# A graph layer on one core: VectorE's work of a step in one fixed order, the spares' slots from one shifted row, and two running extremes

## The chip, the cores and the metric

The kernel runs on one core of one Trainium2 chip. The metric is device time in microseconds (us): the median of the timed runs, 1736.52 us for the kernel before. A profile comes from one execution, whose own time stands beside it.

## The reference, cut to what matters

```python
# N = 12500 nodes, 128 features, E = 400000 edges sorted by dst, edge_type 0 or 1
Xs = x[src]
msg = where(edge_type == 0, Xs @ W_data.T + b_data, Xs @ W_control.T + b_control)
agg = segment_sum(msg, dst, N)
x = layernorm(x + relu(agg + (x @ W_self.T + b_self)))
```

## The kernel before

Sums come first and weights afterwards: for every node the rows of `x` of its incoming edges are added up by edge type, and only these two sums are multiplied by the weights. Rows are held as three bfloat16 parts (`x3` in SBUF, `rows3` in DRAM). The edges are cut into 25 groups of 125 chunks of 128 edges. In a group there are five windows; each has 5 "p" chunks, whose rows GpSimd gathers by indirect DMA (`msg`, L828), and 20 "e" chunks, whose rows are picked out of `x3` by TensorE. A step `w` of the main loop (L1177) handles one such set of 20 e-chunks; there are 107 steps. In a step TensorE does the following, in five units `t` (`picked`, L909):

- it picks rows (`got`, L929) with a one-hot matrix `pick`, ScalarE copies them out as `emsg` (L943), and TensorE adds them up by destination (`sums`, L755), with a one-hot matrix `esel` that VectorE makes in three parts of 10, 9 and 6 cells (1760, 1584 and 1056 elements, `choose`, L918). The tiles `esel` have two buffers;
- in between it adds up the gathered rows with `psel`, counts (L859) and, once a group, multiplies finished sums by the weights (L1048).

Work for later steps runs beside this. For step `w + 2` the slots of the edges are found: each edge has a cell (block of 128 nodes) and needs its rank among the step's edges in that cell. VectorE makes `O` (which cell) and, from `O`, two sums `few` of tens and fives of chunks (L612, L613) and `same` (equal cells in a lane, L602). TensorE counts what lies ahead (`side`, L622). Then comes the **ranks' chain** on VectorE: `ahead` (L630), the product (L634), two folds (L639), `found` (L641), `rank` (L643), `rm` (L533), `rv` (L674). TensorE puts the edges into their slots (`put`, L686), ScalarE copies the result (`cell`, L694), and two DMAs bring it to DRAM and back to all partitions as `pick` (L699), which VectorE turns into the one-hot matrix in the next step (L741). Edges that find no slot are spares: `over` (L645) takes the largest seven of each partition (`key`, `top`, `over_n`, `bits`), TensorE counts over the partitions (L552), VectorE makes `om_all` (L558), TensorE turns it into indices (L562), once for two steps; GpSimd gathers these rows (`both`, L904).

The order of the work comes from three things. Each piece of a step has a place between 0 and 1, and `merged` (L146) records the pieces in the order of their places. The tile framework then orders each engine's queue by these records and by its own estimates of when operands are ready, so VectorE's queue is not simply the recorded order. `issue_after` keeps an instruction behind a named one; before, the work for step `w + 3` and `pick` are only kept behind `rv` (`placed`). Each engine works through its own queue in order.

Where a sum is added into the accumulators `acc` and `cnt` (L817) the column comes from a table: `place_of` (L802) loads ten values into VectorE's registers once a group. `prep` (L473) makes a group's codes and keeps four running extremes (`worst`, L499), which `check_all` (L1102) looks at after the loop.

Of the kernel before, what the change touches and what calls it, by code (L numbers as in the profile page):

```python
# [8 lines left out]
FP = mybir.dt.float32  # L9
# [197 lines left out]
def short_path(ctx, tc, const, ident, eps, wT, brow, bad, x, src, dst, etype, ws, bs, out):  # L207
# [159 lines left out]
    slot_col = keep.tile([P, TOP, OVF], BF, name="slot_col")  # L367
    nc.vector.tensor_copy(slot_col, iota([TOP, OVF], [[-1, TOP], [1, OVF]], 0, 0, "i5"))

    om_all = [keep.tile([P, TOP, 2, OVF], BF, name=f"om_all{k}") for k in range(2)]  # L370
# [15 lines left out]
    worst = keep.tile([P, 5, P], FP, name="worst")  # L386
    nc.vector.memset(worst, 0.0)
# [13 lines left out]
    def places_and_weights():  # L401
# [14 lines left out]
        nc.vector.tensor_reduce(worst[0:1, 4, 0:1], place[:, 0].rearrange("o g w -> o (g w)"), AX.X, OP.max)  # L416
# [56 lines left out]
    def prep(g):  # L473
# [3 lines left out]
        width, high, low = (bounds_of[:GC, v, k:k + 1] for k in range(3))  # L477
        sf = pre.tile([GC, P], FP, name="sf", bufs=1)
        rel = pre.tile([GC, 2, P], FP, name="rel", bufs=1)
# [9 lines left out]
        def rows():  # L489
            near = near_of(g, d)  # L490
            for k in range(2):
                nc.vector.tensor_scalar(rel[:, k], d, near[k], None, op0=OP.subtract)
            nc.vector.tensor_single_scalar(kind, t, 0.0, op=OP.not_equal)
            nc.vector.scalar_tensor_tensor(code[:, 1], kind, width, rel[:, 1], op0=OP.mult, op1=OP.add)
            nc.vector.scalar_tensor_tensor(code[:, 0], kind, float(PW), rel[:, 0], op0=OP.mult, op1=OP.add)
            for k, (most, least) in enumerate(((float(PW - 1), 0.0), (high, low))):
                for j, (end, op) in enumerate(((most, OP.max), (least, OP.min))):
                    w = worst[:GC, 2 * k + j, :]
                    nc.vector.scalar_tensor_tensor(w, rel[:, k], end, w, op0=OP.subtract, op1=op)  # L499
# [29 lines left out]
    def select(sel, col, code2):  # L529

        rows, n, width = sel.shape
        shape = [rows, n, width // 2, 2]
        nc.vector.tensor_tensor(  # L533
            sel.rearrange("p n (w t) -> p n w t", t=2),
            col[:rows].rearrange("p (o w t) -> p o w t", o=1, t=2).to_broadcast(shape),
            code2.rearrange("p n (o t) -> p n o t", o=1).to_broadcast(shape),
            op=OP.is_equal,
        )
        return sel
# [3 lines left out]
    def spare_slots(w, at):  # L543
# [12 lines left out]
        def over_matrix():  # L556
            for k in range(n):
                nc.vector.tensor_scalar(om[:, :, k, :], slot_col, both["before"][:, k:k + 1], None, op0=OP.is_equal)  # L558

        def turn():  # L560
            for j in range(TOP):
                nc.tensor.matmul(  # L562
                    at["rk"][:, col:col + 3 * n], om[:, j].rearrange("p k o -> p (k o)"), both["bits"][:, :, :n, j],
                    start=(j == 0), stop=(j == TOP - 1), skip_group_check=True,
                )

        def keep():
            got = at["rk"][:, col:col + 3 * n].rearrange("p (v k) -> p k v", k=n)
            part = two.tile([P, 2], FP, name="part")
            for k in range(n):  # L570
# [3 lines left out]
                    code, got[half, k, 2:3].rearrange("p (n o) -> p n o", o=1).to_broadcast(list(code.shape))  # L574
                )
                nc.scalar.copy(part[half], got[half, k, :2])
# [6 lines left out]
    def give_slots(w):  # L583
# [5 lines left out]
        def behind():  # L589
            return tc.issue_after(placed[0].ins) if w > 1 else ExitStack()  # L590

        def block_matrix():
            O = s["held"] = two.tile([P, EC * NCELL], BF, name="O")
            s["O"] = O.rearrange("p (c j) -> p c j", j=NCELL)
            select(s["O"], cell_cols[w % 2], blk2)

        def same_lane():
# [3 lines left out]
            with behind():  # L601
                nc.vector.tensor_tensor(  # L602
# [5 lines left out]
        def fours():  # L608
            s["prod"] = big.tile([P, EC, NCELL + EC], BF, name="prod")
            h = s["few"] = s["prod"][:, :, :NCELL]  # L610
            with behind():
                nc.vector.tensor_add(h[:, :2 * CQ], s["O"][:, :2 * CQ], s["O"][:, 2 * CQ:])  # L612
            nc.vector.tensor_add(h[:, 2 * CQ:3 * CQ], h[:, :CQ], h[:, CQ:2 * CQ])  # L613
# [13 lines left out]
        def ranks():  # L627
            ahead = two.tile([P, NCELL], BF, name="ahead")
            with nc.allow_low_precision(reason="whole numbers; those over 256 need not be exact"):
                nc.vector.tensor_reduce(  # L630
                    ahead, s["ahead"][:, :2 * NCELL].rearrange("p (k j) -> p j k", k=2), AX.X, OP.add
                )
            prod = s["prod"]
            nc.vector.tensor_tensor(  # L634
                prod[:, :, :NCELL], s["O"], ahead.rearrange("p (o j) -> p o j", o=1).to_broadcast([P, EC, NCELL]),
                op=OP.mult,
            )
            for h in ((NCELL + EC) // 2, (NCELL + EC) // 4):
                nc.vector.tensor_add(prod[:, :, :h], prod[:, :, :h], prod[:, :, h:2 * h])  # L639
            found = two.tile([P, EC], FP, name="found")  # L640
            nc.vector.tensor_reduce(found, prod[:, :, :h], AX.X, OP.add)  # L641
            rank = s["rank"] = two.tile([P, EC, 2], BF, name="rank")
            nc.vector.tensor_copy(rank, found.rearrange("p (c o) -> p c o", o=1).to_broadcast([P, EC, 2]))  # L643

        def over():  # L645
            key = two.tile([P, EC], FP, name="key")
            nc.vector.scalar_tensor_tensor(key, s["rank"][:, :, 0], CAP - 0.5, pk, op0=OP.is_ge, op1=OP.mult)
# [3 lines left out]
            nc.vector.max(both["top"][:, w % 2, :], key)  # L651
# [18 lines left out]
        def rank_matrix():  # L670
            rm = select(big.tile([P, EC, CAP], BF, name="rm"), rank_col, s["rank"])
            rv = s["rv"] = two.tile([P, EC, 2, CAP], BF, name="rv")
            shape = [P, EC, 2, CAP // 2, 2]
            placed[:] = [nc.vector.tensor_tensor(  # L674
                rv.rearrange("p c v (r t) -> p c v r t", t=2),
                rm.rearrange("p c (o r t) -> p c o r t", o=1, t=2).to_broadcast(shape),
                vals2.rearrange("p c v (o t) -> p c v o t", o=1).to_broadcast(shape),
                op=OP.mult,
            )]
# [49 lines left out]
        if w % 2:  # L729
            s["tiled"][5] = [lambda: (turn_codes(), own_before())]  # L730
            s["own_turn"] = own_turn
        return s, [(0.58, block_matrix), (0.6, fours), (0.66, same_lane)], [
            (0.1, before), (0.31, ranks), (0.35, rank_matrix), (0.75, over),
        ]

    def pick_matrix(w):

        def half(a, b):
            t = slots[w]["pick"][:, a:b].rearrange("p j r -> p (j r)")
            with tc.issue_after(placed[0].ins):  # L740
                nc.vector.tensor_scalar(t, t, lane_f, None, op0=OP.is_equal)  # L741
        return [(0.6, lambda: half(0, NCELL))]


    acc, added, parts_in, at_places = {}, [], {}, {}
# [56 lines left out]
    def place_of(g, i):  # L802

        parts_in[g] = parts_in.get(g, 0) + 1
        if g not in at_places:
            with tc.issue_after(added[-2].ins) if len(added) > 1 else ExitStack():
                _, at_places[g] = nc.values_load_multi_w_load_instructions(
                    raw["place"][0:1, g, :], engines=[nc.vector.engine], min_val=0, max_val=R - WMAX,
# [552 lines left out]
```

## Time and profile before

| what | value |
|---|---|
| median of 3 runs (lowest, highest) | 1736.52 us (1736.14, 1736.97) |
| the profiled execution, its own time | 1736.11 us |
| its span, first to last instruction | 1734.3 us |
| mean granted TensorE clock | 0.992 |
| TensorE (PE) busy | 1569.6 us, 91% |
| VectorE (DVE) busy | 1550.3 us, 89% |
| ScalarE (ACT), GpSimd (POOL) busy | 1246.5 us, 1292.2 us |
| PE in the first 60 us | 6.7 us busy |

A share of busy time is a mean over stages. The first 75 us load and split `x`; from then on all 107 steps look alike, with more work in those in which a group is prepared or finished. PE's busy time is modelled and takes in the 0.17 to 0.33 us that a matmul is on its way, so short waits do not show as idle time.

### The profile page before, as it was taken

Reading aid. Unit: us, or ns where it says so; the run is one execution under the profiler, and the core shown is the slowest. Engines: PE = TensorE matmul, PEld = TensorE weight load, DVE = VectorE, ACT = ScalarE, POOL = GpSimd, SP = SyncE. Lnnn points to the kernel's source line nnn. Section 1 sums busy time; section 2 is a strip of 40 time slices with the busy share of each in tenths; the row PEclk is TensorE's granted clock in tenths of the full one; section 3 lists DMA queues with packets and bytes.
Section 4 is the critical chain, followed back from the end, with each engine's and each line's share of the span. In section 5 each row is a group of like instructions: output and inputs, shape, how many; then the busy total and the mean of one; then the engine's idle time right before and its main releaser. Section 6 shows DMA issues by size and latency. Waiting matters only on the chain.

```text
span 1734.3 us, 67322 instructions
## 1 busy us (share of the span) xinstructions
PE 1569.6 (91%) x28154; PEld 1229.6 (71%) x28154; DVE 1550.3 (89%) x3677; ACT 1246.5 (72%) x2251; POOL 1292.2 (75%) x1061
## 2 busy tenths in 40 slices
PE   0599998999899999999999999999999999999997
PEld 0376777777677777777777777777777777777776
DVE  7898999899798898998998998999998998998983
ACT  5777777677677676777776777776777776777675
POOL 0277888888878788778777787787788787778771
PEclk9999999999999999999999999999999999999999
DMA  7844454444454544454545454445444445444441
GB/s 202 293 130 128 126 154 123 141 151 130 124 157 126 157 136 141 138 157 130 156 131 150 139 150 134 147 117 170 143 148 137 144 137 154 138 145 132 125 126 57
DMA packets 148966, 248.22 MB, mean 143 GB/s; under 512 B 35937, under 2 KB 115260, under 8 KB 148652
## 3 DMA queue, kind: packets, MB, share of 16 engines
q1 hardware_dynamic: 85994, 134.45, 23.4%
q0 software_dynamic: 50032, 102.98, 22.3%
q10 hardware_dynamic: 12626, 6.40, 1.4%
q8 instruction: 222, 3.64, 0.9%
q14 instruction: 92, 0.75, 0.1%
HBM read 226.24 MB, written 17.50 MB: 141 GB/s over the span
## 4 chain that ended last, share of the span: by engine, by line
PE 41%; DVE 39%; ACT 8%; issue 6%; DMA 4%; DVEq 1%; POOL 0%; SPq 0%; ACTq 0%; POOLq 0%
PE sums L755 18%; PE got L929 13%; DVE esel L533 5%; DVE prod L639 4%; ACT emsg L943 4%; PE side L1048 4%; DVE prod L634 3%; DVE pick L741 3%; DVE rv L674 3%; DVE found L641 3%; DVE prod L612 2%; PE side L622 2%; PE side L686 2%; DVE O L533 2%; ACT h L1078 2%
## 5 line engine op out<-in xcount | busy, mean ns | idle before, releaser
L828 POOL DMA_INDIRECT msg<-rows,idx_g x985 | 1222.6, 1241 | 320.4 <-issue 147.2
L943 ACT CAST emsg<-got 128x768 bf16<-128x768 f32 (+1 forms) x1070 | 949.3, 930 | 320.3 <-PE got L929 300.1
L755 PE MATMUL sums<-esel,emsg 128*128 128x176 bf16 x7704 | 693.1, 240 | 3.9 <-DVE acc L817 3.4
L755 PEld LDWEIGHTS <-emsg 128*128 128x128 bf16 x7704 | 566.7, 98 | 117.0 <-issue 108.2
L929 PE MATMUL got<-x,pick 128*32 128x384 bf16 x10486 | 572.9, 330 | 27.7 <-DVE pick L741 13.3
L929 PEld LDWEIGHTS <-pick 128*32 128x32 bf16 x10486 | 242.5, 96 | 155.4 <-issue 24.9
L533 DVE TENSOR_TENSOR esel<-code_col,code 128x1760 bf16<-128x1760 bf16 x321 | 292.1, 910 | 14.5 <-PE sums L755 12.7
L755 PE MATMUL sums<-psel,msg 128*128 128x48 bf16 x2955 | 167.7, 184 | 14.7 <-DVE acc L817 13.0
L755 PEld LDWEIGHTS <-msg 128*128 128x128 bf16 x2955 | 138.8, 97 | 26.8 <-issue 23.7
L639 DVE TENSOR_TENSOR prod<-prod 128x1200 bf16<-128x1200 bf16 x214 | 133.7, 625 | 4.8
L634 DVE TENSOR_TENSOR prod<-O,ahead 128x2000 bf16<-128x2000 bf16 x107 | 128.4, 1200 | 2.5
L533 DVE TENSOR_TENSOR O<-cell_col,blk 128x2000 bf16<-128x2000 bf16 x107 | 127.4, 1191 | 0.9 <-ACT blk L437 0.7
L741 DVE TENSOR_SCALAR pick<-pick,lane_f 128x3200 bf16<-128x3200 bf16 x107 | 113.2, 1058 | 0.8 <-DMA pick<-there 0.8
L817 DVE TENSOR_TENSOR acc<-acc,sums 128x176 f32 (+2 forms) x232 | 66.2, 285 | 52.5 <-PE sums L755 42.2
L904 POOL DMA_INDIRECT both<-rows,idx x54 | 64.2, 1189 | 54.6 <-ACT emsg L943 28.5
L686 PE MATMUL side<-rv,O 128*128 128x64 bf16 x2140 | 83.3, 195 | 21.9 <-DVE rv L674 19.6
L533 DVE TENSOR_TENSOR psel<-near_col,near 128x1200 bf16<-128x1200 bf16 x125 | 95.8, 767 | 0.1
L686 PEld LDWEIGHTS <-O 128*128 128x128 bf16 x2140 | 79.0, 100 | 23.6 <-DVE rv L674 19.8
L674 DVE TENSOR_TENSOR rv<-rm,vals 128x1280 bf16<-128x1280 bf16 x107 | 87.7, 820 | 0.0
L641 DVE TENSOR_REDUCE found<-prod 128x20 f32<-128x600 bf16 x107 | 82.8, 774 | 2.6
L612 DVE TENSOR_TENSOR prod<-O 128x1000 bf16<-128x1000 bf16 x107 | 71.9, 672 | 0.0
L622 PEld LDWEIGHTS <-ltri 128*128 128x128 bf16 x1284 | 41.1, 96 | 38.1 <-issue 36.0
(192 smaller groups left out, 1566.8 us busy)
## 6 DMA issues: line engine op xcount, KB each, us to landing
pick<-there SPq DMA_DIRECT2D x106, 800.0 KB
msg<-rows,idx_g POOLq DMA_INDIRECT x985
acc<-acc_start SPq DMA_DIRECT2D x23, 640.0 KB
rows<-x SPq DMA_DIRECT2D x6, 1344.0 KB
xs<-in_x_dram SPq DMA_DIRECT2D x99, 62.5 KB
out_dram<-h SPq DMA_DIRECT2D x99, 62.5 KB
xt<-in_x_dram ACTq DMA_DIRECT2D x6, 896.0 KB
cnt<-cnt_start SPq DMA_DIRECT2D x22, 160.0 KB
```

The lines of the kernel that those rows point to most:

```text
L533: nc.vector.tensor_tensor(sel.rearrange("p n (w t) -> p n w t", t=2), col[:rows].rearrange("p (o w t) -> p o w t", o=1, t=2).to_broadcast( ...
L612: nc.vector.tensor_add(h[:, :2 * CQ], s["O"][:, :2 * CQ], s["O"][:, 2 * CQ:])
L634: nc.vector.tensor_tensor(prod[:, :, :NCELL], s["O"], ahead.rearrange("p (o j) -> p o j", o=1).to_broadcast([P, EC, NCELL]), op=OP.mult,)
L639: nc.vector.tensor_add(prod[:, :, :h], prod[:, :, :h], prod[:, :, h:2 * h])
L641: nc.vector.tensor_reduce(found, prod[:, :, :h], AX.X, OP.add)
L674: placed[:] = [nc.vector.tensor_tensor(rv.rearrange("p c v (r t) -> p c v r t", t=2), rm.rearrange("p c (o r t) -> p c o r t", o=1, t=2).t ...
L686: nc.tensor.matmul(s["rk"][:m, :2 * CAP], s["held"][:, c * NCELL:c * NCELL + m], s["rv"][:, c].rearrange("p v r -> p (v r)"), start=(c == ...
L741: nc.vector.tensor_scalar(t, t, lane_f, None, op0=OP.is_equal)
L755: last = nc.tensor.matmul(out, msg[:, j * D:(j + 1) * D], sel, start=(start and j == 0), stop=stop, skip_group_check=True)
L828: return nc.gpsimd.indirect_dma_start(out=msg, out_offset=None, in_=rows3[:, :], in_offset=bass.IndirectOffsetOnAxis(ap=codes["p", g][0][: ...
L929: last = nc.tensor.matmul(ps[CAP * a:CAP * (a + 1), :], slots[w]["pick"][:, a * NQ + q, :], x3[:, 4 * q + a - a0].rearrange("p j d -> p (j ...
L943: s["out"] = nc.scalar.copy(msg[:, :n], ps[:, :n, :3 * D])
```

## The change

**A fixed order.** `ranks`, `rank_matrix` and `over` are cut into single operations, each of which returns its instruction. `in_turn` records sixteen of VectorE's operations of a step one behind the other, each with `issue_after` on the one before; work of other kinds (`acc`, `psel`, `prep`, `over`, finishing) still goes between them as the framework sees fit. The two later parts of `esel` are taken out of `picked`'s units into this row.

**Spares.** `slot_col` is one row of 70 numbers instead of 7 x 64, and `om_all` one row of 70 for each of the two steps instead of 7 x 64. The seven positions are seven windows of 128 columns that are shifted by one. A matrix multiply now handles one position of one step (3 columns) instead of one position of both (6 columns): 14 for two steps instead of 7. The two copies of `part` become one.

**Extremes.** `rel` is bfloat16, and `worst` keeps a largest and a smallest value (two operations on 256 elements) instead of four distances (four on 128); the limits are subtracted once at the end.

**Places.** `place_of` loads one value at each use, with a check of its bounds: 232 loads of one value instead of 25 of ten.

```diff
-        def behind():
-            return tc.issue_after(placed[0].ins) if w > 1 else ExitStack()
...
         def over_matrix():
             for k in range(n):
-                nc.vector.tensor_scalar(om[:, :, k, :], slot_col, both["before"][:, k:k + 1], None, op0=OP.is_equal)
+                nc.vector.tensor_scalar(om[:, k, k * OVF:k * OVF + OVF + TOP - 1], slot_col, both["before"][:, k:k + 1], None, op0=OP.is_equal)
 
         def turn():
-            for j in range(TOP):
+            for j in range(n * TOP):
+                k, j = divmod(j, TOP)
+                first = TOP - 1 - j
                 nc.tensor.matmul(
-                    at["rk"][:, col:col + 3 * n], om[:, j].rearrange("p k o -> p (k o)"), both["bits"][:, :, :n, j],
-                    start=(j == 0), stop=(j == TOP - 1), skip_group_check=True,
+                    at["rk"][:, col:col + 3], om[:, k, first:first + P], both["bits"][:, :, k, j],
+                    start=(k + j == 0), stop=(k == n - 1 and j == TOP - 1), skip_group_check=True,
                 )
...
-            for k, (most, least) in enumerate(((float(PW - 1), 0.0), (high, low))):
-                for j, (end, op) in enumerate(((most, OP.max), (least, OP.min))):
-                    w = worst[:GC, 2 * k + j, :]
-                    nc.vector.scalar_tensor_tensor(w, rel[:, k], end, w, op0=OP.subtract, op1=op)
+            for j, op in enumerate((OP.max, OP.min)):
+                nc.vector.tensor_tensor(worst[:GC, v, j], worst[:GC, v, j], rel, op=op)
...
-        if g not in at_places:
-            with tc.issue_after(added[-2].ins) if len(added) > 1 else ExitStack():
-                _, at_places[g] = nc.values_load_multi_w_load_instructions(
-                    raw["place"][0:1, g, :], engines=[nc.vector.engine], min_val=0, max_val=R - WMAX,
...
-        return at_places[g][i]
+        with tc.issue_after(added[-2].ins) if len(added) > 1 else ExitStack():
+            return nc.vector.value_load(raw["place"][0:1, g, i:i + 1], min_val=0, max_val=R - WMAX)
...
+    def in_turn(named, prev=None):
+
+        last = [prev]
+
+        def unit(f):
+            last[0] = f(last[0])
+
+        return [lambda f=f: unit(f) for f in named]
...
+        order = [
+            (0.31, chain.get("ahead")), (0.32, second), (0.33, chain.get("product")), (0.34, chain.get("half")),
+            (0.505, third), (0.51, chain.get("fourth")),
+            (0.515, (lambda prev: pick_matrix(w + 1, prev)) if w + 1 < pairs else None),
+            (0.52, chain.get("found")), (0.53, started("same")), (0.54, chain.get("rank")),
+            (0.55, chain.get("matrix")), (0.56, chain.get("key")), (0.57, chain.get("values")),
+            (0.58, started("blocks")), (0.6, started("tens")), (0.66, started("fives")),
+        ]
+        order = [(at, f) for at, f in order if f]
+        order = [(at, u) for (at, _), u in zip(order, in_turn([f for _, f in order]))]
```

VectorE's queue, the ranks' chain of a step in the middle of the program, before (`prod` is first the product, then the folds, and from L612 on the sums `few` for the next step):

```order
L533 TENSOR_TENSOR esel<-code_col,code 128x1584
L630 TENSOR_REDUCE ahead<-side 128x100
L634 TENSOR_TENSOR prod<-O,ahead 128x20x100
L639 TENSOR_TENSOR prod<-prod 128x20x60
L639 TENSOR_TENSOR prod<-prod 128x20x30
L641 TENSOR_REDUCE found<-prod 128x20
L643 CAST rank<-found 128x40
L533 TENSOR_TENSOR rm<-rank_col,rank 128x640
L533 TENSOR_TENSOR esel<-code_col,code 128x1056
L674 TENSOR_TENSOR rv<-rm,vals_18991 128x1280
L612 TENSOR_TENSOR prod<-O 128x10x100
L602 TENSOR_TENSOR prod<-blk_19455,blk_183 128x20x20
```

And the same queue with the change; the row ahead of these is `ahead` (L638):

```order
L537 TENSOR_TENSOR esel<-code_col,code 128x1584
L644 TENSOR_TENSOR prod<-O,ahead 128x20x100
L652 TENSOR_TENSOR prod<-prod 128x20x60
L537 TENSOR_TENSOR esel<-code_col,code 128x1056
L652 TENSOR_TENSOR prod<-prod 128x20x30
L776 TENSOR_SCALAR pick<-pick,lane_f 128x3200
L657 TENSOR_REDUCE found<-prod 128x20
L606 TENSOR_TENSOR prod<-blk_20248,blk_183 128x20x20
L662 CAST rank<-found 128x40
L537 TENSOR_TENSOR rm<-rank_col,rank 128x640
L669 SCALAR_TENSOR_TENSOR key<-rank,pk 128x20
L704 TENSOR_TENSOR rv<-rm,vals_19783 128x1280
```

The middle part of `esel` (1584), its last part (1056), `pick` and `same` (L606) have moved between `ahead` and `rv`; `O` and `few` for the next step now come behind `rv`.

VectorE's queue where the spares of two steps are handled, before:

```order
L533 TENSOR_TENSOR psel<-near_col,near_18992 128x1200
L651 MAX top<-key 128x8
L656 TENSOR_SCALAR full<-top 128x16
L660 CAST top_i<-top 128x16
L658 TENSOR_REDUCE over_n<-full 128x2
L662 TENSOR_SCALAR bits<-top_i 128x16
L663 TENSOR_SCALAR bits<-top_i 128x16
L666 TENSOR_SCALAR bits<-top_i 128x16
L533 TENSOR_TENSOR esel<-code_col,code 128x1760
L533 TENSOR_TENSOR O<-cell_col_144,blk_21044 128x2000
L558 TENSOR_SCALAR om_all_194<-slot_col,side 128x7x64 x2
```

And with the change; the row ahead of these is `rv` (L704):

```order
L537 TENSOR_TENSOR O<-cell_col_143,blk_21907 128x2000
L677 MAX top<-key 128x8
L537 TENSOR_TENSOR esel<-code_col,code 128x1760
L616 TENSOR_TENSOR prod<-O 128x10x100
L682 TENSOR_SCALAR full<-top 128x16
L686 CAST top_i<-top 128x16
L621 TENSOR_TENSOR prod<-prod 128x5x100
L684 TENSOR_REDUCE over_n<-full 128x2
L688 TENSOR_SCALAR bits<-top_i 128x16
L689 TENSOR_SCALAR bits<-top_i 128x16
L692 TENSOR_SCALAR bits<-top_i 128x16
L562 TENSOR_SCALAR om_all_194<-slot_col,side 128x70 x2
```

`over_n`, for which TensorE waits, now stands behind `O`, the next step's first part of `esel` and `few`; `om_all` follows it directly, where `esel` and `O` stood between before.

235 lines of the change are left out of this document (133 added, 102 removed).

## The prediction

> **What bounds the kernel now.** I read the page first (busy shares, the chain that ended last), then who waited for whom, then the timeline of two steps on TensorE (PE) and VectorE (DVE), then the groups of instructions.
>
> ```profile
> PE 1569.6 (91%) x28154; PEld 1229.6 (71%) x28154; DVE 1550.3 (89%) x3677; ACT 1246.5 (72%) x2251; POOL 1292.2 (75%) x1061
> PE 41%; DVE 39%; ACT 8%; issue 6%; DMA 4%; DVEq 1%; POOL 0%; SPq 0%; ACTq 0%; POOLq 0%
> ```
>
> Two engines are nearly full, and the chain changes between them, with almost equal shares: they work in lockstep, and neither alone sets the end. The waits say where each is late for the other (total, times, longest):
>
> ```profile
> DVE ahead L630 <- PE side L622: 31.9, 50, 2.9
> PE sums L755 <- DVE acc L817: 16.4, 21, 1.8
> PE side L562 <- DVE om_all L558: 14.1, 26, 1.0
> PE got L929 <- DVE pick L741: 13.3, 21, 2.6
> PE side L504 <- DVE code_r L494: 10.4, 15, 0.9
> PE side L552 <- DVE over_n L658: 3.7, 11, 0.7
> PE got L929 <- ACT emsg L943: 12.7, 31, 0.8
> ```
>
> PE waits 57.9 us for DVE in 94 waits (five rows), and DVE waits for PE too, above all at `ahead`. These five rows are the place from which a gain must come. Now PE in a quiet step, from one `side` (L622) to the next, and in the odd step behind it:
>
> ```profile
> 973.70 0.34 PE L562 MATMUL side<-bits_b,om_all 128*128 128x6 bf16 x7
> 973.90 0.31 PE L755 MATMUL sums<-psel,msg 128*128 128x48 bf16 x6
> ...
> 975.06 0.46 PE L622 MATMUL side<-prod,ltri 128*128 128x50 bf16 x12
> ...
> 977.68 1.31 PE L755 MATMUL sums<-esel,emsg 128*128 128x176 bf16 x15
> ...
> 983.26 0.76 PE L686 MATMUL side<-rv,O 128*128 128x64 bf16 x20
> ...
> 987.59 0.46 PE L622 MATMUL side<-prod,ltri 128*128 128x50 bf16 x12
> ...
> 995.69 0.76 PE L686 MATMUL side<-rv,O 128*128 128x64 bf16 x20
> ...
> 997.66 0.18 PE L552 MATMUL side<-over_n,ltri 128*128 128x2 bf16 x1
> ...
> 999.97 0.18 PE L562 MATMUL side<-bits_b,om_all 128*128 128x6 bf16 x1 [0.74 <-DVE om_all L558]
> ```
>
> Between the two `side` PE is never idle: 987.59 - 975.06 = 12.5 us is PE's own work, and such a step can't get shorter by a faster DVE. From the end of `side` (975.52) to `put` (983.26) it takes 7.74 us. 104 steps between 100 and 1690 us make a mean of 15.3 us, so the time lies in the steps with more in them. The same step on DVE:
>
> ```profile
> 975.83 0.35 DVE L630 TENSOR_REDUCE ahead<-side 128x100 bf16<-128x200 f32 x1
> 976.21 1.20 DVE L634 TENSOR_TENSOR prod<-O,ahead 128x2000 bf16<-128x2000 bf16 x1
> 977.45 1.29 DVE L639 TENSOR_TENSOR prod<-prod 128x1200 bf16<-128x1200 bf16 x2
> 978.77 0.78 DVE L641 TENSOR_REDUCE found<-prod 128x20 f32<-128x600 bf16 x1
> 979.59 0.18 DVE L643 CAST rank<-found 128x40 bf16<-128x40 f32 x1
> 979.81 0.49 DVE L533 TENSOR_TENSOR rm<-rank_col,rank 128x640 bf16<-128x640 bf16 x1
> 980.21 0.70 DVE L533 TENSOR_TENSOR esel<-code_col,code 128x1056 bf16<-128x1056 bf16 x1
> 980.83 0.82 DVE L674 TENSOR_TENSOR rv<-rm,vals 128x1280 bf16<-128x1280 bf16 x1
> 981.57 0.67 DVE L612 TENSOR_TENSOR prod<-O 128x1000 bf16<-128x1000 bf16 x1
> 982.16 0.37 DVE L602 TENSOR_TENSOR prod<-blk,blk 128x400 bf16<-128x400 bf16 x1
> 982.45 0.41 DVE L613 TENSOR_TENSOR prod<-prod 128x500 bf16<-128x500 bf16 x1
> 982.77 1.05 DVE L741 TENSOR_SCALAR pick<-pick,lane_f 128x3200 bf16<-128x3200 bf16 x1
> ```
>
> `rv` is done at 981.65, 1.6 us ahead of `put`; `pick` starts 6.9 us after `ahead`. Independent neighbours overlap: L602 starts 0.08 us before the end of L612 (982.24). Dependent ones don't: `rm` starts 0.04 us after the end of `rank` (979.77). A dependent neighbour thus costs 0.12 us more.
>
> **The change part by part: DVE's own work.**
>
> ```profile
> L558 DVE TENSOR_SCALAR om_all<-slot_col,side 128x448 bf16<-128x448 bf16 x107 | 43.0, 439 | 5.3 <-PE side L552 3.7 <-ACT blk L437 0.9 <-ACT emsg L943 0.2
> L666 DVE TENSOR_SCALAR bits<-top_i 128x16 int32<-128x16 int32 (+1 forms) x54 | 9.8, 182 | 0.0
> L792 DVE TENSOR_TENSOR cnt<-cnt 128x140 bf16<-128x140 bf16 x23 | 5.0, 219 | 0.0
> L499 DVE SCALAR_TENSOR_TENSOR worst<-rel,bounds_of,worst 125x128 f32<-125x128 f32 x50 | 15.2, 344 | 0.0
> L499 DVE SCALAR_TENSOR_TENSOR worst<-rel,worst 125x128 f32<-125x128 f32 x50 | 14.1, 283 | 0.0
> L807 DVEq TENSOR_LOAD <-place_i x25: 1064/1320/2315, 75.0 to 1660.8; - x25
> L119 SPq FUSED_REGOPS  x1: 187/187/187, 1713.6 to 1713.6; - x1
> L119 DVEq TENSOR_LOAD <-bad x1: 309/309/309, 1727.6 to 1727.6; - x1
> ...
> 942.09 0.28 DVE L817 TENSOR_TENSOR cnt<-cnt,sums 64x120 f32 x1 [2.05 <-PE sums L755]
> ```
>
> *Neighbours.* In the two orders up to the final check I count 488 places before and 210 now where an instruction waits for the one just ahead of it. 278 x 0.12 us = 33 us less. The product and the first fold, `found` and `same` (it overwrites what `found` read), `rank` and `rm` still stand together.
>
> The Trainium skill ("VectorE: DVE Perf Modes", section "The DRAIN you can't avoid") says that the next VectorE operation does not start until the pipe is empty, and that leaving out semaphores gains nothing; by it these 33 us would be 0. The overlap of L612 and L602 speaks against it here, so I keep 33.
>
> *Spares.* `om_all` with 70 elements lies between 182 ns (16 elements) and 219 ns (140): 0.20 us. 107 x (0.44 - 0.20) = 26 us less.
>
> *Extremes.* 256 bfloat16 elements lie between 219 ns (140) and the 370 ns of L602 (400): 0.28 us, 0.20 with the overlap. 50 of these are 10 us; the 100 before, at 0.31 less 0.08, are 23 us: 13 us less.
>
> *Places.* 25 loads of ten values took 1.06 to 2.3 us, 41 us together if I take half of them at each end. DVE's sequencer does this ahead of the engine, so a part is covered; the 2.05 us behind L791 at 942 are one that is not (at 942 the row names PE, but the load stood there in the order). Half covered would be 20 us of stall. Now there are 232, each 0.31 us, with 0.19 us of register work and a check: about 0.6 us. Ends: 0 if always covered, 139 us if never. Most stand behind an instruction of 0.4 us or more, or ahead of an `ahead` where DVE waits for PE anyway; I take 0.12 us each, 28 us, so 8 us more.
>
> The Trainium skill ("DMA: Bandwidth & Descriptors", section "Latency and other measured facts") gives a floor of about 600 ns for such a load. With it a place would take 0.9 us instead of 0.6, and the upper end, as an estimate from that page, would be 209 us. The 309 ns of L119 on this engine decide.
>
> DVE's work falls by 33 + 26 + 13 - 8 = **64 us**, 0.6 us a step.
>
> **What of it reaches the end: two ledgers.** *PE's.* (a) `pick` now stands in the chain: after `ahead`, the esel of 1584 (about 0.9), product, folds and third esel it starts 4.2 us after `ahead` instead of 6.9. Its 13.3 us go; PE's busy time hides some 0.17 us at each of the 21 waits: -17. What is late there next is the DMA that brings `pick`; it has 2.7 us less, and I leave it at 0, with 15 us as the other end. (b) `code_r` stands one `worst` earlier: half of 10.4 with its hidden part, -6. (c) `acc`: the long loads go and DVE is less full: half of 16.4 with its hidden part, -10. (d) `om_all` takes 0.5 us less for two steps and no longer stands behind `esel` and `O`. But `over_n` does: behind `rv` come `O` 1.1, `esel` 1.0, `few` 0.6 and 0.3 and three short ones, so it ends about 3.2 us after `rv`. PE needs 997.66 - 995.69 = 2.0 us from `put` to L552, and up to 0.4 more where sums stand ahead of it. So it waits some 0.7 us at L552 where it waited 0.74 at L562: 0. (e) Spares' multiplies: 371 more; seven took 973.90 - 973.70 = 0.20 us, 0.028 each: +10.
>
> (f) A new wait. The third `esel` takes the buffer of the first, which is free when the second block of sums ends (977.68 + 1.31 = 978.99, 3.47 us after `side`). DVE would be there after 3.1 us, so it waits. From there: third esel 0.62, fold 0.4, `pick` 0.97, `found` 0.82, `same` 0.29, `rank` 0.22, `rm` 0.40, `key` 0.1, `rv` 0.82: 4.6 us. `rv` ends 8.1 us after `side`, `put` starts at 8.2, where PE is ready at 7.74: +0.48 us. In steps in which sums are multiplied by the weights or codes are prepared (25 groups, two such steps each) PE is later itself; in the other 57 it is 27 us, of which I take 5 off for waits on ScalarE that it covers: +22. Sum of PE's ledger: -17 - 6 - 10 + 10 + 22 = **-1 us**.
>
> *DVE's.* Quiet steps use nothing of the 64 us. The 50 others have 47% of them: **-30 us**. Both ledgers come from the same rows; the first misses what a late DVE costs PE through ScalarE, the second that PE may be full there too. I take the middle, -15 us: 1736.1 - 15 = **1721 us**. The profiled execution's own time, 1736.11, is its span of 1734.3 and 1.8 around it, and is 0.4 below the median of the runs, so the sum holds for the median as well.
>
> **The rivals.** *DVE is the bound in nearly all steps:* the 64 us come through less the 10 us of PE: 1682. For it speak DVE's 89% and PE's five waits; against it the quiet step. *Nothing that can be measured:* PE's ledger alone, 1735. *Slower: `rv` becomes what PE waits for.* Place: `put`, in 57 quiet steps. `psel` (0.69 us with the overlap) and additions stand within the longer chain in about half of them, so the wait is 0.48 + 0.35 = 0.83 us, 47 us; with -33 and +10 that is +24: 1760. It decides from 23 us on, 0.4 us a quiet step, which is near my (f). For it speaks the `put` row with PE ready at 7.74; against it that DVE has 31.9 us of waiting at `ahead` and can begin earlier nowhere else. *The order doesn't help (the neighbours wait all the same):* 33 us less for DVE, so -14 in its ledger, 1728; the two overlapping rows leave little for this, and it is in the second rival's chance.
>
> **How the numbers follow.** Forecast 0.46 (1721, by itself 1700 to 1732); DVE the bound 0.16; no change 0.13; slower 0.25. A measurement of this kernel can tell about 0.2%, 3.5 us, from no change. Faster 0.46 + 0.16 = 0.62, same 0.13, slower 0.25. The range leaves out the lower half of the second case (0.08) and the upper half of the last (0.12): 1685 to 1760; it takes in the 15 us of the DMA and half of what bare loads would cost.
>
> **What would show it.** In the profile after: DVE busy about 1490 us or less; `om_all` near 200 ns; no idle of 2 us before L846; PE's waits on `pick` gone, on `over_n` up, and a new row of PE `side` L717 on `rv`; a DVE wait of the 1056 `esel` on `sums`; 749 instead of 378 multiplies with `om_all`. I am wrong if PE does not wait for `rv` at all (then it should be near 1685), or if that row passes 30 us (then slower), or if DVE idles some 0.5 us behind most of the 232 loads.

## The result, and the profile after

| | before | with the change |
|---|---|---|
| median of 6 runs (lowest, highest) | 1735.88 us (1734.46, 1736.97) | 1750.93 us (1745.59, 1753.44) |
| ratio, 95% interval | | 1.0084 (1.0069 to 1.0099) |
| the profiled execution, its own time | 1736.11 us | 1753.44 us |
| its span | 1734.3 us | 1751.6 us |

The change made the kernel slower, by 15 us; on another chip it was 1.0091 (1.0076 to 1.0106). The profiled execution is the longest of its six, so the profiles differ by 17 us. Ten of the experiments below ran on chips on which the kernel before itself takes 2023 to 2050 us, so every ratio is to the kernel before on the same chip.

The page after, busy time and the chain that ended last:

```profile
PE 1589.1 (91%) x28525; PEld 1249.9 (71%) x28525; DVE 1514.1 (86%) x3630; ACT 1252.3 (71%) x2198; POOL 1295.0 (74%) x1061
DVE 40%; PE 39%; DMA 7%; ACT 6%; issue 6%; DVEq 1%; SPq 0%; ACTq 0%
```

VectorE (DVE) is busy 36 us less than before, yet TensorE (PE) is busy 20 us longer. The added multiplies explain 10 us of that (below); I put the rest down to short waits that its modelled busy time takes in, which is not shown by itself. The waits after (engine, line, waited for: us in total, times, longest):

```profile
DVE esel L537 <- PE sums L789: 62.2, 82, 3.2
DVE ahead L638 <- PE side L630: 51.2, 56, 1.8
PE side L717 <- DVE rv L704: 49.0, 51, 12.4
PE side L556 <- DVE over_n L684: 22.6, 36, 2.4
PE sums L789 <- DVE acc L846: 18.0, 27, 3.3
DVE psel L537 <- issue: 14.6, 22, 1.2
DVE pick L776 <- DMA pick<-there: 14.5, 14, 2.8
DVE acc L846 <- PE sums L789: 14.2, 24, 2.7
PE side L738 <- ACT cell L725: 10.0, 5, 5.7
```

And the rows of before that answer to them and were not shown yet:

```profile
DVE acc L817 <- PE sums L755: 42.2, 35, 7.9
PE side L707 <- ACT cell L694: 25.1, 19, 5.7
PE side L686 <- DVE rv L674: 19.6, 2, 10.8
DVE esel L533 <- PE sums L755: 12.7, 15, 1.4
```

PE's waits for `pick` and `code_r` are gone and `om_all`'s are small, but PE now waits for `rv` 51 times (before twice, both at the start). The first 100 us hold 22.5 us of these 49.0, against 19.6 us before; the other 26.5 us in 48 waits are new. PE also waits for `over_n` 19 us more. VectorE itself waits 62 us where it has to make a part of `esel`, 50 us more than before. A quiet step (one in which no weights are multiplied and no codes transposed) shows both. On VectorE:

```profile
993.70 0.37 DVE L638 TENSOR_REDUCE ahead<-side 128x100 bf16<-128x200 f32 x1 [1.13 <-PE side L630]
993.98 0.99 DVE L537 TENSOR_TENSOR esel<-code_col,code 128x1584 bf16<-128x1584 bf16 x1
...
996.12 0.79 DVE L652 TENSOR_TENSOR prod<-prod 128x1200 bf16<-128x1200 bf16 x1
997.24 0.71 DVE L537 TENSOR_TENSOR esel<-code_col,code 128x1056 bf16<-128x1056 bf16 x1 [0.33 <-PE sums L789]
...
998.25 1.04 DVE L776 TENSOR_SCALAR pick<-pick,lane_f 128x3200 bf16<-128x3200 bf16 x1
...
1001.04 0.83 DVE L704 TENSOR_TENSOR rv<-rm,vals 128x1280 bf16<-128x1280 bf16 x1
```

And on PE:

```profile
993.19 0.47 PE L630 MATMUL side<-prod,ltri 128*128 128x50 bf16 x12
...
1000.37 1.08 PE L789 MATMUL sums<-esel,emsg 128*128 128x176 bf16 x12
1001.92 0.76 PE L717 MATMUL side<-rv,O 128*128 128x64 bf16 x20 [0.47 <-DVE rv L704]
```

The last part of `esel` waits 0.33 us for its buffer, `rv` ends 8.2 us after PE's `side`, and PE idles 0.47 us at `put`.

**Two accounts of 100 steps.** From the records I summed VectorE's busy time (overlaps counted once) and its idle time, from the fifth `side` to the 105th; and, on PE, the time from each matmul's start to the next, put down to the second of the two (so a wait that is hidden in busy time counts too). The kernels e1 to e16 are the experiments below; all those in this table ran where before takes about 1735 us, each in one profiled execution (us). The kernel after and e13 are the same program on two chips, and their sums differ by 6 us, so smaller differences in this table say little.

| kernel | DVE work | DVE idle | sum | idle ahead of `ahead` | of `esel` | of `acc` | of `pick` | PE: `put` | `over_n` | `om_all`'s | `cell`'s |
|---|---|---|---|---|---|---|---|---|---|---|---|
| before | 1418.6 | 135.3 | 1554.0 | 29 | 12 | 46 | 0 | 66.9 | 10.8 | 32.3 | 39.8 |
| after | 1383.4 | 186.3 | 1569.6 | 53 | 59 | 18 | 13 | 108.6 | 30.2 | 29.5 | 22.2 |
| e1 no order | 1398.3 | 134.8 | 1533.1 | 32 | 9 | 31 | 0 | 65.3 | 10.4 | 33.4 | 37.2 |
| e2 order only | 1400.9 | 175.5 | 1576.4 | 63 | 48 | 22 | 14 | 109.9 | 28.4 | 29.0 | 25.5 |
| e3 three buffers | 1387.6 | 182.3 | 1569.9 | 77 | 4 | 24 | 27 | 108.2 | 37.2 | 25.7 | 18.9 |
| e4 ten-value loads | 1375.3 | 204.8 | 1580.1 | 76 | 55 | 29 | 18 | 111.9 | 29.3 | 30.7 | 28.0 |
| e13 after again | 1382.5 | 180.7 | 1563.2 | 52 | 59 | 17 | 9 | 105.6 | 29.8 | 30.0 | 24.1 |
| e14 `pick` late | 1385.0 | 181.0 | 1566.0 | 51 | 58 | 33 | 0 | 76.5 | 41.1 | 32.1 | 37.6 |
| e15 `over` early | 1380.5 | 197.3 | 1577.8 | 56 | 60 | 24 | 17 | 112.0 | 15.1 | 35.7 | 32.1 |
| e16 short row | 1383.1 | 173.0 | 1556.1 | 48 | 63 | 25 | 0 | 72.7 | 5.7 | 62.4 | 45.1 |

Against before, the change takes 35 us of work off VectorE and adds 51 us of idle time: that is the 15.6 us of these 100 steps. On PE the same 15.6 us are +41.7 at `put`, +19.4 at `over_n`, less 17.6 at `cell`'s transposes, 13.2 at `got`, 11.6 where codes are transposed, and smaller terms.

### The profile page after: what moved, and what is told of

It reads as the page before. It is cut to its first block, busy times and chain, and to the rows that moved or that the text cites. A ratio compares the mean times of both kernels' runs of the same rounds, so it can differ in the third digit from the quotient of the medians.

```text
span 1751.6 us, 68660 instructions
## 1 busy us (share of the span) xinstructions
PE 1589.1 (91%) x28525; PEld 1249.9 (71%) x28525; DVE 1514.1 (86%) x3630; ACT 1252.3 (71%) x2198; POOL 1295.0 (74%) x1061
## 4 chain that ended last, share of the span: by engine, by line
DVE 40%; PE 39%; DMA 7%; ACT 6%; issue 6%; DVEq 1%; SPq 0%; ACTq 0%
PE sums L789 18%; PE got L960 12%; DVE esel L537 6%; DMA pick<-there 5%; DVE O L537 4%; DVE found L657 4%; DVE pick L776 3%; DVE rv L704 3%; DVE prod L616 2%; ACT emsg L974 2%; DVE prod L652 2%; DVE rm L537 2%; PE side L1076 2%; PE side L630 2%; DVE prod L606 2%
## 5 line engine op out<-in xcount | busy, mean ns | idle before, releaser
L960 PE MATMUL got<-x,pick 128*32 128x384 bf16 x10486 | 583.4, 331 | 10.1 <-ACT emsg L974 9.0
L960 PEld LDWEIGHTS <-pick 128*32 128x32 bf16 x10486 | 243.0, 96 | 138.8 <-issue 26.9
L789 PEld LDWEIGHTS <-msg 128*128 128x128 bf16 x2955 | 140.4, 97 | 31.6 <-issue 28.4
L776 DVE TENSOR_SCALAR pick<-pick,lane_f 128x3200 bf16<-128x3200 bf16 x107 | 112.2, 1048 | 14.5 <-DMA pick<-there 14.5
L933 POOL DMA_INDIRECT both<-rows,idx x54 | 76.4, 1415 | 58.6 <-ACT emsg L974 45.1
L537 DVE TENSOR_TENSOR psel<-near_col,near 128x1200 bf16<-128x1200 bf16 x125 | 96.8, 775 | 14.9 <-issue 14.6
L704 DVE TENSOR_TENSOR rv<-rm,vals 128x1280 bf16<-128x1280 bf16 x107 | 87.9, 821 | 1.0 <-DVE key L669 1.0
L638 DVE TENSOR_REDUCE ahead<-side 128x100 bf16<-128x200 f32 x107 | 38.9, 364 | 55.0 <-PE side L630 51.2
L725 ACT CAST cell<-side 128x64 bf16<-128x64 f32 x107 | 22.6, 211 | 72.6 <-PE side L717 69.7
```

Source lines behind the costliest of these rows:

```text
L537: ins = nc.vector.tensor_tensor(sel.rearrange("p n (w t) -> p n w t", t=2), col[:rows].rearrange("p (o w t) -> p o w t", o=1, t=2).to_broa ...
L704: placed[:] = [nc.vector.tensor_tensor(rv.rearrange("p c v (r t) -> p c v r t", t=2), s["rm"].rearrange("p c (o r t) -> p c o r t", o=1, t ...
L776: return nc.vector.tensor_scalar(t, t, lane_f, None, op0=OP.is_equal)
L789: last = nc.tensor.matmul(out, msg[:, j * D:(j + 1) * D], sel, start=(start and j == 0), stop=stop, skip_group_check=True)
L933: return nc.gpsimd.indirect_dma_start(out=both[:n, :], out_offset=None, in_=rows3[:, :], in_offset=bass.IndirectOffsetOnAxis(ap=slots[w][" ...
L960: last = nc.tensor.matmul(ps[CAP * a:CAP * (a + 1), :], slots[w]["pick"][:, a * NQ + q, :], x3[:, 4 * q + a - a0].rearrange("p j d -> p (j ...
```

## The experiments

**Which part costs: e1 to e4, one chip, 5 rounds.** Theory A was that the order costs, B the loads, C the multiplies.

e1, without the order (the hunks on spares, extremes and places only; two lines of its difference from the kernel after):

```diff
-        order = [(at, u) for (at, _), u in zip(order, in_turn([f for _, f in order]))]
+            pick_matrix(w + 1) if w + 1 < pairs else [],
```

> The change without its fixed order: the order of before, with the one row of 70 for the spares, the two extremes and the single loads. Theory A (the order costs the time: pick, same and the last part of esel with its wait for a buffer stand between ahead and rv, and TensorE waits 42 us more for rv at put): 1715 to 1732 us, no wait of more than 0.2 us for rv at put in most steps. Theory B (232 single loads stall VectorE, the order is innocent): about 1750 us, as with the whole change. Theory C (371 more small multiplies on TensorE are the cost): 1745 us or more.

Measured: 1717.94 us, 0.9914 (0.9897 to 0.9931). A holds, B and C fall. Its waits:

```profile
DVE ahead L632 <- PE side L624: 32.0, 53, 2.0
PE side L688 <- DVE rv L676: 22.0, 2, 13.2
DVE esel L533 <- PE sums L757: 8.0, 19, 1.3
```

PE waits for `rv` only at the start, and VectorE does not stand at `esel`. This is the fastest kernel of the study.

e2, the order alone (`slot_col` of 7 x 64, four `worst`, ten-value loads):

```diff
-    slot_col = table(OVF + TOP - 1, 1 - TOP, "slot_col")
+    slot_col = keep.tile([P, TOP, OVF], BF, name="slot_col")
```

> The fixed order alone, with the spares, the extremes and the ten-value loads of before. Theory A: 1755 to 1770 us, since the order costs what the whole change lost and the saved work of VectorE is given back; wait for rv at put 40 us or more. Theory B: 1730 to 1740 us. Theory C: below 1740 us.

Measured: 1767.01 us, 1.0192 (1.0174 to 1.0211), as A said. Its row at `put`:

```profile
PE side L715 <- DVE rv L702: 51.0, 50, 9.9
```

The order costs 33.6 us, the other three parts bring 15.4; the difference of 18 is near the 15 of the whole. One thing is not held apart: with another order for VectorE the tile framework also lays some of TensorE's and ScalarE's work in another order (the records of before and of e2 differ there too), and no run keeps those queues fixed.

e3, a buffer for each part of `esel`:

```diff
-            sel = sp.tile([P, 10, 2 * EW], BF, name="esel")[:, :n]
+            sel = sp.tile([P, n, 2 * EW], BF, name=f"esel{n}", bufs=1)
...
-                choose(0, 10)
+                choose(0, 10, placed_o[0])
```

> The whole change, but each of the three parts of esel has a buffer of its own, and the first part is kept behind O, so that VectorE's order stays nearly the same and only the wait of the last part (1056) for its buffer goes (65 us in 90 steps, 0.72 us each). Theory A with the buffer as its main part: rv ends up to 0.7 us earlier, the waits at put fall from 42 us to under 10 us, 1715 to 1730 us. Theory A with the mere length of the row as its main part: the wait moves to another place of the row, 1742 to 1750 us. Theory B: 1748 to 1753 us.

Measured: 1753.21 us, 1.0120 (1.0096 to 1.0144), above both of A's ranges. Its waits:

```profile
DVE ahead L641 <- PE side L633: 77.8, 67, 2.3
PE side L720 <- DVE rv L707: 53.9, 46, 12.4
PE side L556 <- DVE over_n L687: 32.8, 29, 2.4
DVE pick L779 <- DMA pick<-there: 27.7, 23, 2.6
```

The wait for the buffer is gone and nothing is gained: VectorE idles 182 us all the same, now ahead of `ahead` and `pick`. The buffer is not the cause by itself. The time is near Theory B's range (1748 to 1753), but e1 has the single loads too and is faster than before.

e4, the ten-value loads of before:

```diff
-            return nc.vector.value_load(raw["place"][0:1, g, i:i + 1], min_val=0, max_val=R - WMAX)
...
+                _, at_places[g] = nc.values_load_multi_w_load_instructions(
+                    raw["place"][0:1, g, :], engines=[nc.vector.engine], min_val=0, max_val=R - WMAX,
...
+        return at_places[g][i]
```

> The whole change, but with the ten-value loads of before (25 of them instead of 232 single ones). Theory A: 1745 to 1757 us, within 0.4% of the whole change. Theory B: 1730 to 1738 us, as the 20 us go that VectorE idles for issue ahead of psel, acc and cnt.

Measured: 1763.83 us, 1.0165 (1.0145 to 1.0185). Both theories miss it: the single loads are a gain, of about 13 us against the whole change's 1.0084. With ten-value loads VectorE idles 18 to 24 us more than in the two profiles of the whole change, ahead of `ahead` and `acc`.

**Where in the order: e5 to e12.** Theory A is now narrower: the length of the row between `ahead` and `rv` sets the time. Theory A2: VectorE has as much to do wherever it stands, so a wait that is taken away at one place comes back at another. e5 (and e9, e14) puts `pick` behind `rv`, the first edit below; e6 (e10, e15) records `over` right behind `rv`, the second; e8 (e12, e16) makes all three; e7 (e11) is the kernel before with the single loads alone.

```diff
-            (0.515, (lambda prev: pick_matrix(w + 1, prev)) if w + 1 < pairs else None),
+            (0.575, (lambda prev: pick_matrix(w + 1, prev)) if w + 1 < pairs else None),
```

```diff
-            begin = [(0.75, slots[w + 2]["over"])]
+            begin = [(0.572, slots[w + 2]["over"])]
```

```diff
-            (0.52, chain.get("found")), (0.53, started("same")), (0.54, chain.get("rank")),
+            (0.52, chain.get("found")), (0.54, chain.get("rank")),
...
+            (0.577, started("same")), (0.58, started("blocks")), (0.6, started("tens")), (0.66, started("fives")),
```

> The whole change, but pick stands behind rv again (ahead of O) instead of ahead of found. Theory A, length of the row between ahead and rv: the row gets 0.97 us shorter, the waits at put fall from 42 us to under 12 us, some 10 us of waits for pick come back, 1725 to 1738 us. Theory A2, the work only changes places, since VectorE has as much to do in a step wherever it stands (as in the run with three buffers, where the row got 0.6 us shorter and the time stayed): 1745 to 1755 us, with waits for pick, over_n and acc up by what put gives back.

> The whole change, but over is recorded right behind rv, so that top stands ahead of O and over_n ahead of the next first part of esel. Theory A: the 20 us of waits for over_n shrink to under 6 us, the waits at put stay at 40 us or more, 1735 to 1745 us. Theory A2: the time stays at 1745 to 1755 us and put or acc takes up the wait.

> The kernel before with single loads of the places, and nothing else of the change. By the prediction's own term (8 us more work on VectorE, a part of it on the path): 1734 to 1742 us. By what the pair with ten-value loads and with single loads in the fixed order showed (single ones 13 us better): 1720 to 1728 us.

> The whole change, but pick and same stand behind rv and over is recorded right behind rv: between ahead and rv stand only the chain itself and two parts of esel, as before. Theory A: the waits at put fall under 10 us and those for over_n under 6 us, 1712 to 1728 us, about as without any fixed order (1718). Theory A2: 1740 us or more.

Measured, before at 2048.68 us: e5 0.9965 (0.9944 to 0.9986), e6 0.9828 (0.9796 to 0.9861), e7 0.9902 (0.9868 to 0.9936), e8 0.9912 (0.9878 to 0.9946). The page of e8, busy and chain, and its largest wait of PE's queue for weights:

```profile
PE 1693.4 (84%) x28525; PEld 1288.7 (64%) x28525; DVE 1523.8 (75%) x3630; ACT 1255.5 (62%) x2198; POOL 1256.7 (62%) x1061
PE 60%; DVE 15%; ACT 11%; issue 9%; another core or an unknown queue 2%; DMA 2%; DVEq 0%; POOL 0%; SPq 0%; ACTq 0%; POOLq 0%
PEld L960 <- issue: 197.5, 366, 2.4
```

"issue" is time in which PE waited for nothing that the profile shows: 26.9 us on this line in the profile after, 197.5 here. VectorE is busy for 75% of the span and has slack, so these runs can't tell A from A2. The same four kernels on another such chip:

> The whole change, but pick stands behind rv again (ahead of O) instead of ahead of found; once more, since TensorE idled for issue throughout the first time. Theory A, length of the row between ahead and rv: the row gets 0.97 us shorter, the waits at put fall from 42 us to under 12 us, some 10 us of waits for pick come back: 0.990 to 1.002 of before. Theory A2, the work only changes places (as in the run with three buffers): 1.005 to 1.012 of before, with waits for pick, over_n and acc up by what put gives back.

> The whole change, but over is recorded right behind rv, so that top stands ahead of O and over_n ahead of the next first part of esel; once more for the same reason. Theory A: the 20 us of waits for over_n shrink to under 6 us, the waits at put stay at 40 us or more: 0.997 to 1.003 of before. Theory A2: 1.006 to 1.012, and put or acc takes up the wait.

> The kernel before with single loads of the places and nothing else of the change; once more for the same reason. By the prediction's own term (8 us more work on VectorE): 0.999 to 1.004 of before. By what the pair with ten-value loads and with single loads in the fixed order showed (single ones 13 us better): 0.990 to 0.996.

> The whole change, but pick and same stand behind rv and over is recorded right behind rv: between ahead and rv stand only the chain itself and two parts of esel, as before; once more for the same reason. Theory A: the waits at put fall under 10 us and those for over_n under 6 us: 0.985 to 0.995 of before, about as without any fixed order (0.991). Theory A2: 1.002 or more.

Measured, before at 2022.90 us: 0.9982 (0.9960 to 1.0004), 0.9808 (0.9774 to 0.9841), 0.9887 (0.9855 to 0.9919), 0.9916 (0.9886 to 0.9947). By their ratios alone e9 and e12 lie in A's ranges and e10 lies below both, but here too VectorE has slack. Single loads alone are a gain there as well (e7, e11); of the orders, that with `over` early was the best.

**The same edits where VectorE matters: e13 to e16, before at 1734.81 us.**

> The whole change once more, beside the three edits of its order on the same chip. Where TensorE is kept from work by VectorE alone (before about 1735 us): 1.007 to 1.010 of before. Where TensorE idles for issue some 250 us of its own (before above 2000 us), the wait for rv is partly covered by that: 0.985 to 0.995.

> The whole change, but pick stands behind rv again. Where before takes about 1735 us: theory A (length of the row ahead to rv) 0.990 to 1.002 of before, with waits at put under 15 us; theory A2 (the work only changes places) 1.005 to 1.012. Where before takes above 2000 us it was 0.997 and 0.998.

> The whole change, but over is recorded right behind rv. Where before takes about 1735 us: theory A 0.997 to 1.003 of before, the waits for over_n gone and those at put as they were; theory A2 1.006 to 1.012. Where before takes above 2000 us it was 0.983 and 0.981.

> The whole change, but pick and same stand behind rv and over is recorded right behind rv. Where before takes about 1735 us: theory A 0.985 to 0.995 of before; theory A2 1.002 or more. Where before takes above 2000 us it was 0.991 and 0.992.

Measured: e13 (unchanged) 1.0091 (1.0076 to 1.0106); e14 1.0048 (1.0032 to 1.0063); e15 1.0184 (1.0158 to 1.0210); e16 1.0094 (1.0075 to 1.0113). The row of e14 at `put`:

```profile
PE side L717 <- DVE rv L704: 22.9, 6, 12.8
```

`pick` out of the row takes 29 us off `put`, puts 11 on `over_n` and 14 on `cell`'s transposes, and brings 7.6 us by the medians. The table doesn't show these 7.6 us: the profiled execution of e14 was the longest of its five (1748.73 us against a median of 1742.28). In e16 `put` and `over_n` cost nearly what they cost before, and the time is that of e13. Where it went, on VectorE and PE of e16:

```profile
988.75 0.16 DVE L684 TENSOR_REDUCE over_n<-full 128x2 bf16<-128x16 f32 x1
...
989.09 1.19 DVE L537 TENSOR_TENSOR O<-cell_col,blk 128x2000 bf16<-128x2000 bf16 x1
990.20 1.06 DVE L537 TENSOR_TENSOR esel<-code_col,code 128x1760 bf16<-128x1760 bf16 x1
991.18 0.67 DVE L616 TENSOR_TENSOR prod<-O 128x1000 bf16<-128x1000 bf16 x1
...
992.25 0.42 DVE L562 TENSOR_SCALAR om_all<-slot_col,side 128x70 bf16<-128x70 bf16 x1
```

```profile
989.73 0.18 PE L556 MATMUL side<-over_n,ltri 128*128 128x2 bf16 x1
...
992.73 0.51 PE L568 MATMUL side<-bits_b,om_all 128*128 128x3 bf16 x14 [1.43 <-DVE om_all L562]
```

`over_n` is early now, but `O`, `esel` and the tens come ahead of `om_all`, and PE waits for that. Theory A, that the length of the row sets the time, falls as a full cause: e14 and e16 take `put` back almost to before and are not in its ranges. A2 fits e16, where what one place gives back the next takes; e14 (1.0048) lies at the lower edge of its range (1.005 to 1.012) and gives back half of the loss, so there a part of the wait was gained and not only moved. In e15, `over` early alone, the 15 us less at `over_n` came back as +6 at `put`, +6 at `om_all`'s and +8 at `cell`'s, and the kernel got slower still, beyond A2's range (1.006 to 1.012) as well; why it overshot isn't settled. (My expectation of e8 said that two parts of `esel` stood in the row before; there was one, as the quoted order of before shows.)

**Idle time or place: e17 and e18.** e17 is e16 with e3's buffers. e18 keeps a fixed order, with the foreign operations about where before had them (and `over` right behind `rv`); the row of its order:

```diff
+            (0.29, second), (0.31, chain.get("ahead")), (0.33, chain.get("product")), (0.34, chain.get("half")),
+            (0.51, chain.get("fourth")), (0.52, chain.get("found")), (0.54, chain.get("rank")),
+            (0.55, chain.get("matrix")), (0.555, third), (0.56, chain.get("key")), (0.57, chain.get("values")),
+            (0.573, (lambda prev: pick_matrix(w + 1, prev)) if w + 1 < pairs else None),
+            (0.575, started("same")), (0.7, started("blocks")), (0.72, started("tens")), (0.74, started("fives")),
```

> The short row (pick and same behind rv, over recorded behind rv) and a buffer for each part of esel, with the first part kept behind O. In the short row alone TensorE no longer waited at put, but VectorE stood idle 68 us for the buffer of the last part of esel, and TensorE waited for om_all, which came behind O and esel, and for acc. Theory E (a row that may not be left turns a wait of VectorE into lost work, and TensorE gets it back at the next thing that VectorE owes it): with that idle time gone om_all and acc come earlier, 0.990 to 1.002 of before. Theory F (any order in which O and the first part of esel stand behind rv is this slow): 1.006 or more. Where before takes above 2000 us it can't tell.

> A fixed order of the same sixteen operations, but with the foreign ones where the kernel before had them: the middle part of esel ahead of ahead, the last behind rm, pick, same, O, tens and fives behind rv, over right behind rv. Theory E: no wait of VectorE for the buffer of the last part above 15 us, waits at put under 5 us, 0.985 to 0.997 of before (without a fixed order 0.991). Theory F: 1.003 or more. Where before takes above 2000 us it can't tell.

Measured, before at 2050.02 us: 0.9870 (0.9841 to 0.9899) and 0.9954 (0.9936 to 0.9971), on a chip on which PE idled for issue: they can't tell. It stays open which fixed order, if any, keeps VectorE's idle time at the 135 us of the free ones.

## Why the prediction was wrong, by its steps

The measured 1750.93 us lies inside the range, but the sign is wrong. The third rival (`rv` becomes what PE waits for, 1760 us, with a chance of 0.25) is what came at `put`; e16 shows that this was a place of the cost and not the whole of it. Its 47 us at `put` are near the 41.7 measured, but it had 57 steps at 0.83 us, and there are 68 at 0.6. That its sum comes within 10 us is in part luck: it left out the 19.4 us at `over_n` and the 17.6 us saved at `cell`'s transposes, which nearly cancel.

- **The step that failed is "I take the middle".** PE's ledger gave -1 us, VectorE's -30, and I averaged them, as if the work saved were passed on and VectorE's idle time stayed. It rose by 51 us. Without the order it did stay (134.8 us), and there 20 us less work are 21 us less time: for three parts of the change the work came through almost whole (by the medians 15 us), as the first rival had it, and not by the 47% of VectorE's ledger. Neither ledger had the idle time that the fourth part, the order, adds. In PE's ledger the same failure is two terms, (f) and (d).
- **(f), the wait for `rv`: right in one step, too small in sum.** 0.48 us a quiet step was forecast, 0.47 stands in the quiet step above; but `put` takes 41.7 us more instead of 22. It starts within 0.1 us of the end of `rv` in 68 of the 100 steps: in 51 of the 60 quiet ones and in all 17 in which codes are transposed and no weights multiplied. These 17 I had left out, because I took PE to be late there. In the 23 steps with weights PE is late indeed, and `put` starts 2.2 us or more after `rv` on average. Over the 68 steps the 41.7 us are 0.6 us each. The row that the prediction names as a sign (over 30 us means slower) reads 49.0, though 22.5 of these lie in the first 100 us.
- **(d), `over_n` and `om_all` put at 0:** +19.4 at `over_n` and -2.8 at `om_all`'s multiplies, which contain the added ones.
- **(c), `acc` at -10:** missed; that row went from 16.4 to 18.0 us.
- **(a), `pick`:** its waits on PE went as forecast, and `got` takes 13 us less (-17). Its DMA, left at 0 with 15 us as the other end, made VectorE wait 14.5 us inside the row.
- **(b) and (e):** codes -11.6 us (-6 forecast). 749 multiplies at 27 ns in the median take 10 us more than before's 378, as forecast.
- **Neighbours: 33 us forecast, 15 to 18 measured** as less work (after against e1, e2 against before); the gaps of 34 ns that go besides are some 10 us of idle time. The count was about right: between 100 and 1690 us, 481 starts of before lie 30 to 40 ns behind their predecessor's end, and 184 of after. But not each overlap is a gain, as two groups show, first before and then after:

```profile
L643 DVE CAST rank<-found 128x40 bf16<-128x40 f32 x107 | 20.0, 187 | 2.4
L662 DVE TENSOR_SCALAR bits<-top_i 128x16 int32<-128x16 int32 (+1 forms) x54 | 10.8, 201 | 0.0
L662 DVE CAST rank<-found 128x40 bf16<-128x40 f32 x107 | 28.2, 264 | 0.0
L688 DVE TENSOR_SCALAR bits<-top_i 128x16 int32<-128x16 int32 (+1 forms) x54 | 15.0, 277 | 0.0
```

`rank` now starts under `same` and takes 77 ns longer. The Trainium skill ("VectorE: DVE Perf Modes", section "The DRAIN you can't avoid") says that the next operation waits for an empty pipe, but adds that one which is not held starts earlier. The prediction left that addition out, and so read the section as saying that the order would save nothing. The starts about 80 ns ahead of a predecessor's end agree with the addition, and the work saved in e2 (1418.6 to 1400.9) shows that the saving is not 0.
- **Spares and extremes:** `om_all` and `worst` after:

```profile
L562 DVE TENSOR_SCALAR om_all<-slot_col,side 128x70 bf16<-128x70 bf16 x107 | 23.6, 259 | 3.0 <-PE side L556 2.3
L499 DVE TENSOR_TENSOR worst<-worst,rel 125x256 bf16<-125x256 bf16 x50 | 14.0, 285 | 0.0
```

`om_all` went from 43.0 to 23.6 us of busy time (26 less forecast), `worst` from 29.3 to 14.0 (13 less forecast). In all VectorE is busy for 1514.1 us, where about 1490 or less was forecast; `om_all` and the neighbours gave less than reckoned.
- **Places: the sign was wrong.** I charged 8 us; e4 against the whole change shows a gain of 13 us. The loads after:

```profile
L840 DVEq TENSOR_LOAD <-place_i x232: 298/304/1670, 43.8 to 1739.7; - x116
L840 DVEq FUSED_REGOPS  x232: 183/190/206, 44.7 to 1740.0; - x116
```

Load, registers and check take about 0.52 us, and VectorE's waits for issue come to 22 us (`psel` 14.6, the rest in small rows). As sums of stalls my charges were near: from 100 us on, VectorE stands idle during 25 us of the long loads in e4 (20 charged) and during 26 us of the single loads, registers and checks after (28 charged). So the gain of 13 us doesn't lie in the sum of these stalls. e4 shows that a long load costs more than its stall; how it does so stays open. The Trainium skill ("DMA: Bandwidth & Descriptors", section "Latency and other measured facts") gives about 600 ns as the least for such a load; the median of 304 ns over 232 loads here is half of it, and the measurement decides.

## What to carry to other kernels

Where two engines wait for each other twice in a step, charge a change of one engine's order in that engine's work plus its idle time, and ask of each place where it may not go on what could have been done there: fixed rows forbid just that. A wait that is gone shows its place, not its worth; the sum over a step tells whether it went or moved. Test a bundle's parts alone: here three of four were worth 15 us, and the fourth cost 33.

## What the runs showed of the hardware

- An instruction on VectorE that starts 80 ns before its predecessor's end may end no earlier: `rank` took 264 ns instead of 187, three operations on 16 elements 277, 248 and 211 instead of 201, 191 and 182.
- On three of the chips the same kernel before takes 2023 to 2050 us instead of 1735. The granted clock of these runs is 0.96 to 0.98 instead of 0.99, too little for 17%. The kernels profiled there (not before itself) show 156 to 226 us of "issue" ahead of `got`'s weights, against 27 us in the profile after. Of the three edits `over` early is the fastest there (0.983 and 0.981 of before) and the slowest where PE does not idle so (1.018). What holds PE back there the profile doesn't show.
